# Cross-attention, eight sequences on one core: half of the partition swaps of quads 24 to 56 issued by GpSimd

## The chip, the cores and the metric

The kernel runs on one core of a Trainium2 chip. The metric is device time in microseconds of one execution; three runs of the kernel before gave 575.96, 576.25 and 576.99, a median of 576.25 us.

The engines are named here as in the profile: PE is TensorE (matmuls; PEld is its weight loads), DVE is VectorE, ACT is ScalarE, POOL is GpSimd, SP is SyncE, which in this kernel only issues transfers (its queue is SPq).

## The reference

Everything is float32. A layer norm of x, a projection to queries, attention of 32 heads of width 32 over 256 keys, an output projection and the residual. Keys and values are both the context itself, without a projection.

```python
mu = mean(x); var = variance(x)                      # x: (8, 256, 1024)
h = (x - mu) * rsqrt(var + 1e-5) * gamma + beta
Q = split_heads(h @ Wq.T)                            # 32 heads of 32
K = split_heads(ctx); V = split_heads(ctx)           # ctx: (8, 256, 1024)
scores = einsum('bhsd,bhtd->bhst', Q, K) * 32 ** -0.5
probs = softmax(where(mask, scores, -inf))
attn = einsum('bhst,bhtd->bhsd', probs, V)
out = x + merge_heads(attn) @ Wout.T
```

## The kernel before

**Quads.** The work of attention is cut into 64 quads: sequence b (0 to 7) times group (0 to 7) of four heads, numbered n = 8 b + group. One pass of the main loop, step n, puts on TensorE: the scores of quad n + 1 (L486), the values of quad n - 2 (L629), and between and behind them the query projection of a later sequence (L447, from the fourth sequence on in seven products per sequence, Strassen-like) and steps of the output projection of an earlier one (L715). It then emits the softmax of quad n + 1 (`softmax_parts`). The order of instructions on each engine is the order in which the program is written; each engine executes its own list in that order and waits on semaphores.

**One softmax.** For each of the four heads j of a quad: `exps(j)` is bias, minimum over the row on VectorE (L522) and exponential with row sum on ScalarE (L526), for two halves of the rows each; `normalize(j)` is a reciprocal of the row sums on VectorE (L533) and two scalings of 128 x 256 on GpSimd (L535); `blocks(j)` is one transpose in blocks of 32 x 32 on VectorE (L541), which writes the head's part of the tile pT. VectorE works through the reciprocals and transposes of one quad before the bias and minimum of the next, so the scalings on GpSimd stand between them.

**The swaps.** Blocks of 32 x 32 transposed in place leave the keys of two neighbouring groups of 32 partitions in the wrong halves. So partitions 32 to 63 of half 0 have to change places with partitions 0 to 31 of half 1, and 96 to 127 with 64 to 95. `aside(0)` and `aside(1)` on ScalarE (L547) copy half 1 of pT to a tile pc, two heads at a time; then, in `tail()`, two transfers of 128 KB inside the on-chip memory overwrite half 1 from half 0 (L607, "pT<-pT"), and two more write half 0 from pc (L611, "pT<-pc"). The first two wait for the second copy aside; each of the other two waits for the landing of the first of its pair, which reads what it overwrites. Loads that happen to be due (`between`: keys, residual rows, kept weights, the next x) are issued between the two pairs. All of this goes through SyncE's queue, which waits in order. pT has three buffers, pc two; the scores have four banks, one quad's worth, so the scores of quad n + 1 need the bias and minimum of quad n done.

**What else GpSimd does.** Behind the scalings of a quad stand, in the order of the program: sums for the query products (`sum_x`, L437), sums for the output products (`sum_at`, L691), additions to the residual (`add_p1`, L748; `add_kept` near the end), and small layer norm steps (L239, L249). In the first sequences it also folds gamma into the weights and forms weight sums (L366, L185, L398).

**Where tails are deferred.** In the first eight quads and in quads 57 to 62, `tail()` runs after the next quad's first exponentials; in quads 8 to 56, and 63, directly behind the scalings.

Of the kernel before, what the change touches and what calls it, by code (L numbers as in the profile page):

```python
# [59 lines left out]
def xattn_kernel(  # L60
# [11 lines left out]
    nc = tc.nc  # L72
# [4 lines left out]
    NQ = NC  # L77
# [4 lines left out]
    K = 32  # L82
# [4 lines left out]
    N = B * NQ  # L87
# [403 lines left out]
    def softmax(*args):  # L491
        for _ in softmax_parts(*args):
            pass

    tails = []


    def softmax_parts(n, copies=(), ahead=(), between=(), hooks={}, fill=()):

        fill = list(fill)

        def fill_in():
            if fill:
                fill.pop(0)()

        pss = scs[n]  # L510
        pT = pTs[n] = ptp.tile([P, 2, NI, NH, NS, K], F32, tag="pT", name=f"pT_{n}")
        pc = asp.tile([P, NI, NH, NS, K], F32, tag="pc", name=f"pc_{n}")
        es, mns, dens = {}, {}, {}

        def exps(j, part=range(NS)):
            if 0 in part:
                es[j] = ep.tile([P, NS, T], F32, tag="e", name=f"e_{n}_{j}")
                mns[j] = sm.tile([P, NS], F32, tag="mn", name=f"mn_{n}_{j}")
                dens[j] = sm.tile([P, NS], F32, tag="den", name=f"den_{n}_{j}")
            e, mn, den = es[j], mns[j], dens[j]  # L520
            for s in part:
                nc.vector.tensor_tensor_reduce(  # L522
                    out=e[:, s, :], in0=pss[j][:, s, :], in1=mbs[n // NQ], scale=1.0,
                    scalar=NO_SCORE, op0=ALU.add, op1=ALU.min, accum_out=mn[:, s : s + 1],
                )
                nc.scalar.activation(  # L526
                    e[:, s, :], e[:, s, :], AF.Exp, bias=mn[:, s : s + 1], scale=-1.0,
                    accum_out=den[:, s : s + 1],
                )

        def normalize(j):
            rden = sm.tile([P, NS], F32, tag="rden", name=f"rden_{n}_{j}")
            nc.vector.reciprocal(rden, dens[j])  # L533
            for s in range(NS):
                nc.gpsimd.tensor_scalar(  # L535
                    es[j][:, s, :], es[j][:, s, :], rden[:, s : s + 1], 1.0,
                    ALU.mult, ALU.mult,
                )

        def blocks(j):  # L540
            nc.vector.transpose(  # L541
                pT[:, :, :, j, :, :].rearrange("p a i s k -> p (a i) s k"),
                es[j].rearrange("p s (b t) -> p b s t", t=K),
            )

        def aside(j):
            nc.scalar.copy(pc[:, :, ts(j, 2)], pT[:, 1, :, ts(j, 2)])  # L547

        if n == 0:
            for j in range(NH - 1):  # L550
                exps(j, (0,))
            yield
            exps(NH - 1, (0,))
            fill_in()
            yield
            for j in range(NH):
                exps(j, (1,))
            normalize(0)
            fill_in()
        else:  # L560
            exps(0)
            while tails:
                tails.pop()()
            late = "p1" in hooks
            if not late:
                for done in list(pvs):
                    copy_at(done)
            exps(1)
            for hook in hooks.get("soon", ()):
                hook()  # L570
            exps(2)
            normalize(0)
            for hook in hooks.get("p1", ()):
                hook()
            exps(3)
            if late:
                for done in list(pvs):
                    copy_at(done)
        if n <= NQ:
            for copy in copies:  # L580
                copy()
        for hook in hooks.get(0, ()):
            hook()
        normalize(1)
        fill_in()
        blocks(0)
        for hook in hooks.get(1, ()):
            hook()
        normalize(2)
        fill_in()  # L590
        blocks(1)
        aside(0)
        normalize(3)
        fill_in()
        blocks(2)
        while fill:
            fill_in()
        if n > NQ:
            for copy in copies:
                copy()  # L600

        def tail():
            blocks(3)
            aside(1)

            for r in range(2):
                nc.sync.dma_start(pT[ts(2 * r, K), 1], pT[ts(2 * r + 1, K), 0])  # L607
            for load in between:
                load()
            for r in range(2):  # L610
                nc.sync.dma_start(pT[ts(2 * r + 1, K), 0], pc[ts(2 * r, K)])  # L611

        for load in ahead:
            load()
        if n < NQ or N - NQ < n < N - 1:
            tails.append(tail)
        else:
            tail()
        yield
# [16 lines left out]
    def copy_at(n):  # L636
        b, c = divmod(n, NQ)
        k, c = divmod(c, NK)
        if c == 0:
            ats[b, k] = atp.tile([P, NK, NS, NA, K], F32, tag="at", name=f"at_{b}_{k}")  # L640
        for r, pv in enumerate(pvs.pop(n)):
            nc.scalar.copy(
                ats[b, k][:, c, :, ts(r, 2), :], pv.rearrange("p a s k -> p s a k")
            )
# [243 lines left out]
    for c in range(NC):  # L888
        copy_x0(1, c, nc.scalar if c < NC // 2 else nc.vector)
    first = softmax_parts(0, (partial(copy_q, 1), partial(copy_q, 2)), (), (), {}, [  # L890
        partial(ln_stats, 1, 0), partial(ln_stats, 1, 1),
        partial(ln_norm, 1, 0, nc.vector),
# [14 lines left out]
    for b in range(B - 1):  # L907
        done, ends = 0, b == B - 2
        for i, counts in enumerate(steps_of(b)):
            n = NQ * (b + 1) + i  # L910
# [227 lines left out]
```

## Time and profile before

| | |
|---|---|
| median of three runs | 576.25 us |
| profiled execution, span | 577.0 us |
| TensorE busy | 567.3 us, 98% |
| VectorE busy | 460.4 us, 80% |
| ScalarE busy | 411.7 us, 71% |
| GpSimd busy | 409.8 us, 71% |
| DMA queue of SyncE | 110.40 MB, 66.8% of 16 DMA engines' span |
| DMA queue of GpSimd | not in the profile |

The span runs from the first to the last instruction of the profiled execution, which was 0.75 us longer than the median of the runs. Busy time counts instructions that compute; issuing a transfer, semaphore and register instructions are not in it. A timeline row gives start and duration in us, engine, line, operation, output and input tiles (buffer numbers left out), shape, how many instructions were merged into the row (x8), and in brackets the idle time in front of it with what ended it. A row by stretches gives, for each engine, busy time and number of instructions, then the granted TensorE clock (1.00 is full), the DMA engines' busy share and GB/s. A row of waits reads: who waited, for whom, total us, times, longest.

### The profile page before, as it was taken

Reading aid. Unit: us, or ns where it says so; the run is one execution under the profiler, and the core shown is the slowest. Engines: PE = TensorE matmul, PEld = TensorE weight load, DVE = VectorE, ACT = ScalarE, POOL = GpSimd, SP = SyncE. Lnnn points to the kernel's source line nnn. Section 1 sums busy time; section 2 is a strip of 40 time slices with the busy share of each in tenths; the row PEclk is TensorE's granted clock in tenths of the full one; section 3 lists DMA queues with packets and bytes.
Section 4 is the critical chain, followed back from the end, with each engine's and each line's share of the span. In section 5 each row is a group of like instructions: output and inputs, shape, how many; then the busy total and the mean of one; then the engine's idle time right before and its main releaser. Section 6 shows DMA issues by size and latency. Waiting matters only on the chain. (4 is left out here: it accounts for less than half of the span.)

```text
span 577.0 us, 20128 instructions
## 1 busy us (share of the span) xinstructions
PE 567.3 (98%) x7162; PEld 394.2 (68%) x7162; DVE 460.4 (80%) x1695; ACT 411.7 (71%) x1425; POOL 409.8 (71%) x677
## 2 busy tenths in 40 slices
PE   8999998999999999999999999999999999999997
PEld 8788784667667777677676677667766767755543
DVE  5888887788877879979888788988878878779823
ACT  4697886677667877688677867768767776769810
POOL 1778898889896896876568675676658657448770
PEclk9999999899999999999999999999999999999999
DMA  8974766656677777957678856687567864446751
GB/s 304 394 206 126 208 161 180 192 148 166 185 220 222 200 208 207 271 166 201 188 213 228 211 138 189 212 240 206 148 161 236 224 170 130 130 138 178 199 166 73
DMA packets 50100, 111.69 MB, mean 194 GB/s; under 512 B 9424, under 2 KB 10192, under 8 KB 50000
## 3 DMA queue, kind: packets, MB, share of 16 engines
q1 hardware_dynamic: 49712, 110.40, 66.8%
q8 instruction: 57, 0.93, 0.7%
q14 instruction: 43, 0.35, 0.2%
q10 hardware_dynamic: 288, 0.01, 0.0%
HBM read 60.04 MB, written 10.49 MB: 122 GB/s over the span
## 5 line engine op out<-in xcount | busy, mean ns | idle before, releaser
L535 POOL TENSOR_SCALAR e<-e,rden 128x256 f32<-128x256 f32 x512 | 236.0, 478 | 116.9 <-DVE rden L533 114.4
L526 ACT ACTIVATE e<-e,mn 128x256 f32<-128x256 f32 x512 | 253.9, 501 | 50.7 <-DVE mn L522 49.6
L541 DVE STREAM_TRANSPOSE pT<-e 128x512 f32<-128x512 f32 x256 | 180.9, 707 | 44.7 <-POOL e L535 32.7
L522 DVE CUSTOM_DVE_ANT_0 e<-sc,mb 128x256 f32<-128x256 f32 x512 | 185.4, 416 | 26.4 <-PE sc L486 26.0
L547 ACT COPY pc<-pT 128x512 f32<-128x512 f32 x128 | 79.0, 617 | 72.1 <-DVE pT L541 36.6
L526 ACT ACTIVATION_READ_ACCUMULATOR e<-e,mn 128x1 f32 x512 | 97.9, 191 | 0.0
L345 PE MATMUL pq<-xnT,wq 128*128 128x256 f32 (+1 forms) x368 | 84.1, 383 | 0.6 <-ACT qa L354 0.6
L345 PEld LDWEIGHTS pq<-xnT,wq 128*128 128x128 f32 x368 | 68.9, 190 | 15.4 <-issue 3.7
L629 PE MATMUL pv<-pT,v 64*32 64x128 f32 x4096 | 74.7, 274 | 3.5 <-DMA v<-in_kv_dram 2.9
L629 PEld LDWEIGHTS pv<-pT,v 64*32 64x32 f32 x4096 | 57.5, 105 | 26.7 <-issue 14.7
L486 PEld LDWEIGHTS sc<-k,qa 32*128 32x128 f32 x1024 | 46.2, 184 | 41.9 <-issue 23.6
L715 PE MATMUL po_S<-wo,at 128*128 128x512 f32 x152 | 74.3, 606 | 0.0
L486 PE MATMUL sc<-k,qa 32*128 32x256 f32 x1024 | 73.6, 401 | 0.1
L715 PE MATMUL po_A<-wo,at 128*128 128x512 f32 x128 | 61.2, 620 | 0.3 <-ACT qa L354 0.3
L715 PE MATMUL po_S<-wo,s 128*128 128x512 f32 x104 | 49.9, 606 | 0.0
L533 DVE RECIPROCAL rden<-den 128x2 f32<-128x2 f32 x256 | 37.6, 147 | 7.7 <-ACT e L526 6.8
L522 DVE DVE_READ_ACCUMULATOR2_ANT mn<- 128x1 f32 x512 | 42.5, 83 | 0.0
L715 PEld LDWEIGHTS po_A<-wo,at 128*128 128x128 f32 x128 | 23.4, 193 | 26.2 <-issue 24.5
L447 PEld LDWEIGHTS pq_A<-xnT,wq 128*128 128x128 f32 x320 | 37.3, 192 | 4.8 <-issue 3.6
L715 PEld LDWEIGHTS po_S<-wo,at 128*128 128x128 f32 x152 | 25.8, 190 | 19.7 <-issue 19.1
L447 PE MATMUL pq_A<-xnT,wq 128*128 128x128 f32 x320 | 37.3, 275 | 0.0
L748 POOL TENSOR_TENSOR r<-r,p 128x512 f32<-128x512 f32 x23 | 29.4, 1278 | 7.1 <-DMA r<-in_x_dram 3.3
(96 smaller groups left out, 608.7 us busy)
## 6 DMA issues: line engine op xcount, KB each, us to landing
v<-in_kv_dram SPq DMA_DIRECT2D x64, 256.0 KB, 3.9
pT<-pT SPq DMA_DIRECT2D x128, 128.0 KB, 3.1
pT<-pc SPq DMA_DIRECT2D x128, 128.0 KB, 3.5
ring<-kept_T SPq DMA_DIRECT2D x18, 512.0 KB, 5.2
k<-in_kv_dram SPq DMA_DIRECT2D x32, 256.0 KB, 3.1
x<-in_x_dram SPq DMA_DIRECT2D x14, 512.0 KB, 5.1
r<-in_x_dram SPq DMA_DIRECT2D x28, 256.0 KB, 5.1
out_dram<-r SPq DMA_DIRECT2D x28, 256.0 KB, 3.0
```

Source lines behind the costliest of these rows:

```text
L345: nc.tensor.matmul(pqs[n], wq[:, o, c, :], xnTs[b](c), start=(c == 0), stop=(c == NC - 1),)
L447: nc.tensor.matmul(pqs[b][:, o, :], w[:, c], x_[:, c], start=begins and o + c == 0, stop=c == NK - 1, skip_group_check=True,)
L486: nc.tensor.matmul(scs[n][j][:, s, :], qa[r, n % NQ, ts(s, P)], ks[n - n % 2][r, n % 2, :], start=True, stop=True,)
L522: nc.vector.tensor_tensor_reduce(out=e[:, s, :], in0=pss[j][:, s, :], in1=mbs[n // NQ], scale=1.0, scalar=NO_SCORE, op0=ALU.add, op1=ALU.m ...
L526: nc.scalar.activation(e[:, s, :], e[:, s, :], AF.Exp, bias=mn[:, s : s + 1], scale=-1.0, accum_out=den[:, s : s + 1],)
L533: nc.vector.reciprocal(rden, dens[j])
L535: nc.gpsimd.tensor_scalar(es[j][:, s, :], es[j][:, s, :], rden[:, s : s + 1], 1.0, ALU.mult, ALU.mult,)
L541: nc.vector.transpose(pT[:, :, :, j, :, :].rearrange("p a i s k -> p (a i) s k"), es[j].rearrange("p s (b t) -> p b s t", t=K),)
L547: nc.scalar.copy(pc[:, :, ts(j, 2)], pT[:, 1, :, ts(j, 2)])
L629: nc.tensor.matmul(pvs[n][r][j * HD : (j + 1) * HD], vs[n][ts(r, 2 * K), i, ts(j, HD)], pT[ts(r, 2 * K), :, i, j, :, :], start=(i == 0), s ...
L715: nc.tensor.matmul(po, operand(b, name)[:, c], wo[:, which, c], start=begins and c == 0, stop=c == NK - 1, skip_group_check=not begins,)
L748: nc.gpsimd.tensor_tensor(r, r, p1s[b], ALU.add)
```

## The change

In `tail()` the four swaps become calls of a helper `swap(r, back, engine)`: r is the pair (0: partitions 0 to 63, 1: partitions 64 to 127), `back` tells the write of half 0 from pc from the write of half 1 from half 0. Pair 0 stays on SyncE's queue at the same places. For quads 24 to 56 pair 1 is issued by GpSimd: its first swap at the place in the program where SyncE's stood, so in GpSimd's order directly behind the quad's last scaling and ahead of the sums and additions of that step; its second swap is put into a list and issued in the next quad's softmax, in GpSimd's order between the two scalings of `normalize(0)` and those of `normalize(1)`. In all other quads both pairs go through SyncE as before. 66 transfers change their queue; number and size of transfers, and everything on TensorE, VectorE and ScalarE, stay in the same order.

```diff
     tails = []
+    shared = []
+    FIRST_SHARED, LAST_SHARED = 3 * NQ, N - NQ + 1
...
             exps(2)
             normalize(0)
+            while shared:
+                shared.pop()()
             for hook in hooks.get("p1", ()):
                 hook()
             exps(3)
...
             aside(1)
 
-            for r in range(2):
-                nc.sync.dma_start(pT[ts(2 * r, K), 1], pT[ts(2 * r + 1, K), 0])
+            def swap(r, back, engine):
+                to, of = (pT[ts(2 * r + 1, K), 0], pc[ts(2 * r, K)]) if back else (
+                    pT[ts(2 * r, K), 1], pT[ts(2 * r + 1, K), 0]
+                )
+                engine.dma_start(to, of)
+
+            second = nc.gpsimd if FIRST_SHARED <= n < LAST_SHARED else nc.sync
+            swap(0, False, nc.sync)
+            swap(1, False, second)
             for load in between:
                 load()
-            for r in range(2):
-                nc.sync.dma_start(pT[ts(2 * r + 1, K), 0], pc[ts(2 * r, K)])
+            swap(0, True, nc.sync)
+            if second is nc.sync:
+                swap(1, True, second)
+            else:
+                shared.append(partial(swap, 1, True, second))
```

NQ is 8 and N is 64, so `FIRST_SHARED` is 24 and `LAST_SHARED` 57.

## The prediction

> **What bounds the kernel now.** I read the waits and the busy time by stretches first, since they say whether anything but TensorE sets the end, then one quad's timeline on each engine, then the rows that price the moved transfers. The stretch in which quads 24 to 56 are scaled and swapped runs from about 217 to 500 us; inside it I take two batches of eight quads each.
>
> ```profile
> core 0: us, PE busy (x) PEld busy (x) DVE busy (x) ACT busy (x) POOL busy (x), PEclk, DMA share, GB/s
> 217.00:500.00 283.00, 282.15 (x3871) 200.02 (x3878) 236.39 (x870) 210.84 (x740) 189.30 (x327) 1.00 0.70 195
> ...
> 284.82:352.75 67.93, 67.93 (x922) 48.06 (x921) 58.21 (x213) 51.39 (x179) 45.96 (x81) 1.00 0.73 200
> 421.70:489.63 67.93, 67.93 (x922) 48.06 (x921) 53.36 (x203) 49.21 (x177) 44.38 (x77) 1.00 0.67 189
> ...
> PE pv L629 <- DMA v<-in_kv_dram: 0.9, 1, 0.9
> ```
>
> TensorE is busy for 282.15 of 283.00 us, at a granted clock of 1.00, and waited once, 0.9 us, for a load of v. Both batches take exactly 67.93 us, all of it TensorE's. So in this stretch nothing can be won beyond 0.85 us; the change can only keep TensorE fed or starve it. GpSimd has 67.93 - 45.96 = 21.97 us to spare in the first batch. The question is what the change does with that spare time.
>
> One quad, quad 34, whose scores TensorE makes at 300.98, shows where it lies. Engine by engine, in the order GpSimd, VectorE, ScalarE, SyncE's queue, TensorE:
>
> ```profile
> 304.62 3.92 POOL L535 TENSOR_SCALAR e<-e,rden 128x256 f32<-128x256 f32 x8 [0.78 <-DVE rden L533]
> 308.50 1.27 POOL L691 TENSOR_TENSOR s<-at,at 128x512 f32<-128x512 f32 x1
> 309.74 1.26 POOL L437 TENSOR_TENSOR xnT<-xnT,sx 128x512 f32<-128x512 f32 x1
> ...
> 313.56 3.67 POOL L535 TENSOR_SCALAR e<-e,rden 128x256 f32<-128x256 f32 x8
> ...
> 308.57 0.71 DVE L541 STREAM_TRANSPOSE pT<-e 128x512 f32<-128x512 f32 x1 [0.27 <-POOL e L535]
> ...
> 313.27 0.42 DVE L522 CUSTOM_DVE_ANT_0 e<-sc,mb 128x256 f32<-128x256 f32 x1
> ...
> 309.32 0.62 ACT L547 COPY pc<-pT 128x512 f32<-128x512 f32 x1 [1.01 <-DVE pT L541]
> ...
> 309.96 1.14 SPq L607 DMA_DIRECT2D pT<-pT  x2
> ...
> 314.70 1.14 SPq L611 DMA_DIRECT2D pT<-pc  x2
> ...
> 316.04 1.88 PE L715 MATMUL po_S<-wo,s 128*128 128x512 f32 x4
> 317.86 1.15 PE L486 MATMUL sc<-k,qa 32*128 32x256 f32 x16
> ...
> 328.30 1.16 PE L629 MATMUL pv<-pT,v 64*32 64x128 f32 x64
> ```
>
> The eight scalings end at 308.54. The last transpose and the copy aside end at 309.28 and 309.94, and only then may the first swap be issued: 1.40 us after the last scaling, the "turn". During the turn GpSimd now goes straight on with its additions (308.50, 309.74). The last bias-and-minimum of quad 35, at 313.27 + 0.42 = 313.69, frees the last score bank; TensorE writes the next scores at 317.86. So the softmax chain may come 4.17 us late before TensorE feels it, once; whatever it loses after that, TensorE loses too.
>
> **The change, part by part.** *Work moved to GpSimd.* For each of 33 quads two transfers of 128 KB leave SyncE's queue for GpSimd's. Bytes are the same. Before, SyncE takes 1.14 us for two such issues, 0.57 each.
>
> GpSimd has no transfer in this trace, so its price S for issuing one has to be bounded. GpSimd's additions, its smallest instruction and the landing of these swaps:
>
> ```profile
> L607 SPq DMA_DIRECT2D pT<-pT x68: 507/582/1892, 218.7 to 499.6; - x68
> DMA to landing us min/median/max: 2.2/3.4/6.5
> ...
> 295.00 0.55 POOL L239 TENSOR_TENSOR rstd<-ve,mhalf 128x1 f32<-128x1 f32 x1 [2.43 <-DVE ve L236]
> 317.20 0.26 POOL L249 TENSOR_SCALAR shift<-mv,rstd 128x1 f32<-128x1 f32 x1
> 317.42 1.27 POOL L691 TENSOR_TENSOR at<-at,s 128x512 f32<-128x512 f32 x1
> 321.43 0.93 POOL L535 TENSOR_SCALAR e<-e,rden 128x256 f32<-128x256 f32 x2 [2.73 <-DVE rden L533]
> 335.12 1.27 POOL L748 TENSOR_TENSOR r<-r,p 128x512 f32<-128x512 f32 x1
> 351.94 1.27 POOL L691 TENSOR_TENSOR at<-at 128x512 f32<-128x512 f32 x1
> ```
>
> The low end is GpSimd's smallest instruction, 0.26 us (one value a partition); the high end its dearest, 1.27. The nearest row is the same transfer's issue on SyncE, 0.57, and a GpSimd instruction also pays its own start, for which the 0.26 stands: I take 0.57 + 0.27 = 0.84 us, an estimate from these two rows. [...]
>
> *The first swap on GpSimd, and the wait in front of it.* It stands directly behind the last scaling in GpSimd's order and waits for the copy aside. GpSimd executes in order, so each quad's additions, and behind them the next quad's scalings, queue behind the turn: 1.40 us in which GpSimd used to work or wait for something else, plus S.
>
> *The swap back, behind the next quad's first scaling.* It costs S again, and it waits for the first swap to land. SyncE's swaps land a median 3.4 us after their issue starts; with the dearer issue 3.4 + 0.27 = 3.67. On GpSimd's side S, the quad's additions X and a pair of scalings (0.93) pass meanwhile: 1.77 + X. With two or three additions the landing is covered. It is not in four quads of the batch: that with X = 0.55 (row at 295.00) waits 1.35, those with X = 1.27 (335.12, 351.94) 0.63 each, that with 0.26 + 1.27 (317.20, 317.42) about 0.41, together 3.0. Queued behind that wait are the other six scalings, and behind them VectorE's transposes.
>
> *The sum for a batch of eight.* GpSimd's own work 45.96, eight turns 11.20, sixteen issues 13.44, landing waits 3.0: 73.6 us against TensorE's 67.93. GpSimd becomes the bound, by 5.7 us per batch. Quads 24 to 47 are three such batches (189.30 us in 283 is 45.4 per 67.93, so the shown one is no outlier): 17.1. Quads 48 to 55 have 1.58 us less on GpSimd (44.38): 4.1. Quad 56 adds an eighth of a batch, 0.7. Together 21.9, less the 4.17 that the chain may be late: 17.7 us. The profiled execution spans 577.0 us, 0.75 above the median of the runs, 576.25; put on the median, 576.25 + 17.7 = 594.0.
>
> *What is late next.* When the chain is late it is VectorE's bias-and-minimum that frees the score banks late, so TensorE waits at the scores (L486). The sums for the products have about as much room: the one made at 308.50 is used at 316.04, 6.3 us after its end, and would be made 1.40 + 0.84 = 2.2 us later, leaving 4.0. The values are not late: SyncE's second swap back for quad 34 is issued at about 315.3, lands near 318.7, and TensorE reads it at 328.30; GpSimd's would land 1 to 2 us later plus the lag.
>
> *SyncE's queue.* It is spared 66 issues of 0.57, 38 us. What it waited for is here:
>
> ```profile
> SPq L607 <- ACT pc L547: 44.7, 18, 5.1
> SPq L611 <- DMA pT<-pT: 39.9, 32, 2.9
> ```
>
> Both waits stay, since the other half's swaps stay there; loads behind them go up to 1.14 us earlier. Costed at a gain of nothing, as TensorE's only wait for a load is the 0.9 above; with it the gain is 0.9. The buffers hold: three of pT, two of pc, and the next use of pc is two quads (17 us) on.
>
> **The rivals.**
> 1. *GpSimd's issue is no dearer than SyncE's*: the batch is then 60.2 + 16 S, and up to S = 0.55 it exceeds 67.93 by no more than 1.0, which the 4.17 covers over 33 quads: 576.3. At 0.57 the sum is still within a few tenths. For it: GpSimd's smallest instruction is only 0.26. Against it: 0.55 is below SyncE's own price for the same transfer.
> 2. *GpSimd's issue costs 1 us or more*: at 1.0 the batch is 76.2 and the time 604; at 1.27, the dearest instruction that GpSimd has here, 80.5 and about 622. Against it: 1.27 is the price of 512 elements on all partitions.
> 3. *VectorE holds the issue up*: if each issue waited for one VectorE instruction, 0.42 us as at 313.27, S would be 1.26 and the time about 621. Against it: the eight scalings take 3.67 to 3.92 us beside running VectorE work. [...]
> 4. *Faster*: SyncE's relief brings the load of v in time, 0.9 us, 575.4. It decides only if S stays under 0.55; and the 0.85 us of idle TensorE leave no room for more than 0.2% (1.15 us, about what a measurement of this kernel can tell from no change), unless TensorE's instructions get shorter.
>
> **How the numbers follow.** My forecast, S between 0.55 and 1.0, gets 0.40 with its own range 577 to 604; rival 1 0.21; rival 2 0.26; rival 3 0.08; rival 4 beyond 0.2% 0.05. Slower is 0.40 + 0.26 + 0.08 = 0.74, the same 0.21, faster 0.05. The range goes down to 575.4 (the 0.9 us) and up to 612 (S = 1.12), which leaves out the dear half of rivals 2 and 3, about 0.17, and little below.
>
> **What would show it.** Right: two transfer issues per quad on GpSimd of 0.7 to 1.0 us; the additions starting some 2.2 us after the last scaling instead of at once; GpSimd's wait for VectorE's reciprocals (L533), 2 to 3 us in most quads, mostly gone; VectorE's wait for scores gone and TensorE waiting at the scores for VectorE from about quad 30 on; batches of 70 to 75 us instead of 67.93. Wrong: batches still of 67.93 with issues under 0.55; or the lag showing on the values instead, which would mean a landing far beyond 6.5 us; or issues over 1 us, where the mechanism holds and the price fails.

## The result, and the profile after

The changed kernel takes 600.12 us (median of four runs, 598.80 to 602.72) against 576.11 for the kernel before: a ratio of 1.0417, 95% interval 1.0381 to 1.0452. That is 24.0 us slower; the forecast was 594.0, range 575.4 to 612. The profiled execution took 600.83 us, 0.7 above the median; its span, from the first to the last instruction, is 599.1, that is 1.7 less. The 577.0 us given ahead of the prediction is a span too, so by an estimate from this difference that execution took about 578.7 us and stood 2.5 above its median instead of 0.75.

First the busy time of the page of the kernel after and its stretches (columns as in the prediction: busy time and number of instructions for each engine, granted clock, DMA share, GB/s). 214.13 to 521.85 us holds the work that stood between 217 and 500 us before, the stretch in which the swaps are shared (both ends shifted by the starts of the same quads' scores); 287.18 to 362.61 runs from the scores of quad 32 to those of quad 40, the batch that took 67.93 us before; the last two rows are a wait of TensorE and what follows it.

```profile
PE 572.9 (96%) x7162; PEld 394.4 (66%) x7162; DVE 458.6 (77%) x1695; ACT 412.1 (69%) x1425; POOL 445.5 (74%) x743
```

```profile
214.13:521.85 307.72, 289.90 (x3870) 201.55 (x3878) 234.81 (x870) 211.57 (x740) 224.01 (x391) 0.98 0.63 179
287.18:362.61 75.43, 70.23 (x922) 48.59 (x921) 58.04 (x213) 51.62 (x180) 54.57 (x97) 0.98 0.65 183
320.00:323.20 3.20, 0.11 (x2) 0.00 (x0) 1.81 (x11) 3.10 (x13) 3.20 (x5) 0.93 0.31 84
323.20:326.60 3.40, 3.35 (x7) 1.19 (x7) 2.29 (x6) 0.86 (x3) 3.35 (x8) 0.57 0.63 193
```

For the same work TensorE now needs 307.72 us instead of 283: it idles 17.82 us where it idled 0.85, and is busy for 289.90 instead of 282.15. The batch takes 75.43 us; the prediction said 73.6. GpSimd is busy 54.57 us in it instead of 45.96, and the 8.61 more are sixteen issues of 0.54, which the profile, other than with SyncE's issues, counts as busy time (x97 instead of x81).

What GpSimd waited for in that batch, and its rows around the end of quad 34 and the start of quad 35 (timeline: start, duration, engine, line, operation; in brackets the idle time ahead and what ended it):

```profile
POOL pT L614 <- ACT pc L549: 12.3, 7, 2.0
POOL e L537 <- DVE rden L535: 3.5, 3, 1.6
POOL pT L614 <- DMA v<-in_kv_dram: 2.0, 1, 2.0
POOL pT L614 <- DMA pT<-pT: 1.8, 2, 1.1
```

```profile
317.64 0.54 POOL L614 DMA_DIRECT2D pT<-pT  x1 [1.69 <-ACT pc L549]
318.21 1.29 POOL L705 TENSOR_TENSOR s<-at,at 128x512 f32<-128x512 f32 x1
319.45 1.26 POOL L437 TENSOR_TENSOR xnT<-xnT,sx 128x512 f32<-128x512 f32 x1
320.67 0.56 POOL L239 TENSOR_TENSOR rstd<-ve,mhalf 128x1 f32<-128x1 f32 x1
321.21 1.26 POOL L762 TENSOR_TENSOR r<-r,p 128x512 f32<-128x512 f32 x1
322.46 0.93 POOL L537 TENSOR_SCALAR e<-e,rden 128x256 f32<-128x256 f32 x2
323.34 0.60 POOL L614 DMA_DIRECT2D pT<-pc  x1
323.99 2.75 POOL L537 TENSOR_SCALAR e<-e,rden 128x256 f32<-128x256 f32 x6
```

The first swap waits 1.69 us for the copy aside, the turn. It adds up over the batch to 14.3 us (12.3, and 2.0 put down to a load at the same place). Busy 54.57, turns 14.3 and landings 1.8, the terms of the prediction's sum, make 70.7 of the 75.43 us. The rest is 3.9 us of other waits, 3.5 of them for VectorE's reciprocals (18.2 before), and small gaps. So GpSimd has little slack left, but its own list does not fill the batch. Where does TensorE feel the delay? Its own waits in the kernel after, from 217 to 530 us:

```profile
PE po_S L729 <- DVE r L771: 14.2, 7, 3.1
PE po_A L729 <- DVE qa L463: 2.0, 2, 1.2
PE sc L486 <- DVE qa L468: 1.2, 3, 0.4
```

Not at the scores (1.2 us), but at the output products, L729, for VectorE's store L771 that empties the bank of an earlier product. One of the seven waits, on VectorE and TensorE:

```profile
322.50 0.69 DVE L771 TENSOR_TENSOR r<-po_A,r 128x512 f32<-128x512 f32 x1 [1.39 <-POOL r L762]
...
316.38 3.73 PE L447 MATMUL pq_S<-sx,ring 128*128 128x128 f32 x32
323.25 3.41 PE L729 MATMUL po_S<-wo,s 128*128 128x512 f32 x4 [3.13 <-DVE r L771]
326.58 1.15 PE L486 MATMUL sc<-k,qa 32*128 32x256 f32 x16
```

GpSimd adds to the residual (L762, 321.21 to 322.47), the last of the four instructions that queue behind the turn and the issue; VectorE's store waits 1.39 us for that; TensorE's products wait 3.13 us for the store, so VectorE would have been late without the addition too. Then the four products take 3.41 us instead of the 1.88 of the prediction's row at 316.04, since the clock granted in 323.20 to 326.60 is 0.57. Three such stores in the kernel before, each with the product behind it (the product of the second row is that row at 316.04):

```profile
247.21 0.69 DVE L757 TENSOR_TENSOR r<-po_A,r 128x512 f32<-128x512 f32 x1 [1.44 <-POOL r L748]
...
313.62 0.69 DVE L757 TENSOR_TENSOR r<-po_A,r 128x512 f32<-128x512 f32 x1
...
348.23 0.69 DVE L757 TENSOR_TENSOR r<-po_S,r 128x512 f32<-128x512 f32 x1
...
248.12 1.88 PE L715 MATMUL po_S<-wo,s 128*128 128x512 f32 x4
...
350.08 2.74 PE L715 MATMUL po_S<-wo,s 128*128 128x512 f32 x6
```

The room there is 248.12 - 247.90 = 0.22, 316.04 - 314.31 = 1.73 and 350.08 - 348.92 = 1.16 us. Such a store stands ahead of quads 28, 36, 44 and 52 (room 0.22, 1.73, 0.68 and 1.59 us in this trace) and ahead of quads 32, 40 and 48 (1.16 or 1.17): these are the seven waits of 14.2 us. At quad 28 the store already waited 1.44 us for the addition before the change.

Setting the starts of each quad's scores in the two traces against each other, TensorE falls behind by 3.6, 4.8, 3.4 and 4.5 us at quads 28, 36, 44 and 52, by 1.4, 1.1 and 1.9 at 32, 40 and 48, and by 24.7 in all from quad 22 on (up to there the trace after is 2.9 us ahead); behind quad 52 by nothing more. So 20.7 of the 24.7 us come at the seven stores, longer products behind three of them included. The rest has other places: 0.7 each at 33, 41 and 49, where TensorE waits 0.41 us for VectorE in the middle of the scores ahead (sc <- qa above), and 0.9 at 35, where it waits for VectorE at po_A.

### The profile page after: what moved, and what is told of

It is laid out like the page before. It is cut to its first block, busy times and chain, and to the rows that moved or that the text cites. A ratio compares the mean times of both kernels' runs of the same rounds, so it can differ in the third digit from the quotient of the medians.

```text
span 599.1 us, 20193 instructions
## 1 busy us (share of the span) xinstructions
PE 572.9 (96%) x7162; PEld 394.4 (66%) x7162; DVE 458.6 (77%) x1695; ACT 412.1 (69%) x1425; POOL 445.5 (74%) x743
## 4 chain that ended last, share of the span: by engine, by line
PE 55%; POOL 18%; DVE 10%; DMA 7%; issue 5%; ACT 3%; SPq 1%; POOLq 0%; DVEq 0%; ACTq 0%
PE po_S L729 13%; POOL e L537 10%; PE pq L345 9%; PE pq_A L447 8%; PE sc L486 7%; PE pv L643 6%; PE po_A L729 6%; DVE e L524 4%; DVE pT L543 3%; DMA pT<-pT 3%; ACT e L528 2%; DMA v<-in_kv_dram 2%; PE po_end L796 2%; POOL pT L614 2%; PE pq_S L447 2%
## 5 line engine op out<-in xcount | busy, mean ns | idle before, releaser
L549 ACT COPY pc<-pT 128x512 f32<-128x512 f32 x128 | 78.9, 617 | 98.5 <-issue 43.4
L345 PEld LDWEIGHTS pq<-xnT,wq 128*128 128x128 f32 x368 | 68.7, 190 | 14.3 <-issue 4.1
L729 PE MATMUL po_S<-wo,at 128*128 128x512 f32 x152 | 74.5, 607 | 0.2 <-DVE r L767 0.2
L729 PE MATMUL po_S<-wo,s 128*128 128x512 f32 x104 | 55.1, 660 | 14.2 <-DVE r L771 14.2
L614 POOL DMA_DIRECT2D pT<-pT x33 | 17.9, 543 | 59.0 <-ACT pc L549 57.0
L729 PE MATMUL po_A<-wo,at 128*128 128x512 f32 x128 | 59.5, 605 | 2.2 <-DVE qa L463 2.0
L535 DVE RECIPROCAL rden<-den 128x2 f32<-128x2 f32 x256 | 37.3, 146 | 13.3 <-ACT e L528 12.1
L729 PEld LDWEIGHTS po_A<-wo,at 128*128 128x128 f32 x128 | 22.9, 189 | 27.7 <-issue 24.0
L729 PEld LDWEIGHTS po_S<-wo,s 128*128 128x128 f32 x104 | 19.2, 202 | 33.1 <-issue 16.8
L729 PEld LDWEIGHTS po_S<-wo,at 128*128 128x128 f32 x152 | 25.8, 190 | 20.2 <-issue 19.5
```

The source lines that it names most:

```text
L345: nc.tensor.matmul(pqs[n], wq[:, o, c, :], xnTs[b](c), start=(c == 0), stop=(c == NC - 1),)
L614: engine.dma_start(to, of)
L729: nc.tensor.matmul(po, operand(b, name)[:, c], wo[:, which, c], start=begins and c == 0, stop=c == NK - 1, skip_group_check=not begins,)
```

## The experiments

No kernel here leaves out work of the reference. A loss is the ratio less 1, times 576 us. "The first swap" and "the back swap" are those of partitions 64 to 127 in quads 24 to 56. Lines carry each kernel's own numbers: the first swap's and back swap's line is L614 or L616, the copy aside L547 or L549, the addition to the residual and VectorE's store move likewise.

### One of the two moves alone

The back swap left to SyncE:

```diff
-            second = nc.gpsimd if FIRST_SHARED <= n < LAST_SHARED else nc.sync
...
-            if second is nc.sync:
-                swap(1, True, second)
-            else:
-                shared.append(partial(swap, 1, True, second))
+            swap(1, True, nc.sync)
```

> Only the first swap (half 1 of partitions 64 to 127) is issued by GpSimd, the swap back stays on SyncE. Theory A (the loss comes from the turn: GpSimd stands still until the copy aside, the addition of P1 behind it comes late, VectorE's store of the first result block waits for that addition, and TensorE waits for the bank): nearly the whole loss of the changed kernel remains, 592 to 600 us. Theory B (the loss comes from GpSimd's issuing time, 0.55 us for each of 66 transfers): half of it goes, about 588. Theory C (my prediction's sum, GpSimd's total of work, turns and issues): one issue of 0.55 us per quad less, 33 x 0.55 = 18 us less, about 582.

585.51 us, 1.0174 (1.0148 to 1.0201): a loss of 10.0. None of the three theories had this time: it lies between B's and C's.

The first swap left to SyncE, the back swap behind the next quad's first scalings as in the change:

```diff
-            swap(1, False, second)
+            swap(1, False, nc.sync)
```

> Only the swap back is issued by GpSimd, behind the next quad's first scaling; the first swap stays on SyncE, so GpSimd doesn't wait for the copy aside. Theory A: the loss goes nearly, 576 to 579 us. Theory B: half of it stays, about 588. Theory C: GpSimd's sum for eight quads is 46 + 8 x 0.55 = 50 us against TensorE's 67.9, so the loss goes, 576.

595.94 us, 1.0345 (1.0272 to 1.0418): a loss of 19.9. Each half alone loses much; their sum, 29.9, is above the 24.0 of both, so the second kernel did something that the change does not. All three theories had expected 576 to 588 us. TensorE's longest waits and GpSimd's wait for the landing in it (217 to 530 us):

```profile
PE po_A L729 <- DVE qa L463: 8.1, 4, 3.0
...
POOL pT L614 <- DMA pT<-pT: 17.8, 14, 2.8
```

The back swap now waits 17.8 us for SyncE's first swap to land, where the changed kernel waits 8.6 in the same window; another 16.4 us of idle time ahead of it are put down to other engines, so the wait may be up to twice as long. So it is no clean half of the change: it prices a landing wait in the middle of a quad's scalings. TensorE feels this one mostly at other places, 8.1 us at po_A and 4.6 at the scores, both for VectorE's qa, and only 2.5 at the stores.

### The wait without the issue

All swaps on SyncE; GpSimd makes a copy of one value a partition (0.18 us) from the tile of the copy aside, at the first swap's place:

```diff
             aside(1)
+            if 3 * NQ <= n < N - NQ + 1:
+                nc.gpsimd.tensor_copy(gs[:, :1], pc[:, NI - 1, NH - 1, NS - 1, K - 1 : K])
```

> All swaps on SyncE as before the change; at the place of the first swap GpSimd copies one value per partition out of the copy aside's output, so it only waits there, for about 0.3 us of work. Theory A: the additions come 1.7 us (the wait) plus 0.3 late instead of 1.7 plus 0.55, and half or more of the loss stays, 586 to 596 us. Theories B and C: no transfer is issued by GpSimd, eight turns of 1.7 us fit into its spare time (46 + 13.6 + 2.4 = 62 us of 67.9), 576 to 577.

576.88 us, 1.0033 (1.0010 to 1.0057): a loss of 1.9. The turn is there in full, 53.6 us over 33 quads, and most of it goes into time that GpSimd had waited for reciprocals (88.5 us in this window before, 41.3 here):

```profile
POOL gs L606 <- ACT pc L547: 53.6, 33, 2.1
POOL e L535 <- DVE rden L533: 41.3, 41, 4.7
...
PE po_S L717 <- DVE r L759: 2.5, 3, 1.3
```

The last row is TensorE's: its waits at the output products are there already, but small. The time is the one of theories B and C; A, by which the turn alone costs 586 to 596, is wrong.

### Is it the addition to the residual?

The largest wait came behind that addition, at the quads 28, 36, 44 and 52, each of which is scored behind the softmax of quad 26, 34, 42 or 50. First those four quads were given back to SyncE:

```diff
-            second = nc.gpsimd if FIRST_SHARED <= n < LAST_SHARED else nc.sync
+            second = nc.gpsimd if FIRST_SHARED <= n < LAST_SHARED and n % NQ != 2 else nc.sync
```

> As the changed kernel, but the four quads whose swap stands ahead of the addition of P1 to the first result block (26, 34, 42, 50) keep all swaps on SyncE. Theory A: the four lags of 3.4 to 4.8 us that TensorE shows right behind them go, and with them their cause, 580 to 585 us. Theories B and C: 29 of 33 quads still pay, 29/33 of 24 us, about 597.

591.72 us, 1.0283 (1.0258 to 1.0309): a loss of 16.3, 7.7 less than the change. The lag at quads 28, 36, 44 and 52 fell to 0.7, 1.9, 1.9 and 0.5 us, but 1.9 each remain at 32, 40 and 48. The time lies between the 580 to 585 of theory A and the 597 of the others.

Then the addition itself was taken off GpSimd:

```diff
-        nc.gpsimd.tensor_tensor(r, r, p1s[b], ALU.add)
+        engine = nc.vector if (s, h) == (0, 0) and b > 1 else nc.gpsimd
+        engine.tensor_tensor(r, r, p1s[b], ALU.add)
```

> As the changed kernel, but the addition of P1 to the first result block, which VectorE's store waits for, is done by VectorE itself from the third sequence on (one addition of 0.7 us in a batch of eight quads), so it no longer queues behind GpSimd's swap. Theory A (that store is the place where TensorE loses most, 3.4 to 4.8 us once per batch): those four lags shrink to 1 to 2 us, 586 to 591 us. Theory C (GpSimd's total is the bound): only 1.27 us less for GpSimd per batch, 595 to 597.

604.49 us, 1.0475 (1.0431 to 1.0518): worse still, and above both forecasts. The lags at the same four quads are 4.4, 5.1, 5.1 and 3.6. TensorE's largest wait stays, with another name, and VectorE's addition and the store behind it show why this kernel settles less than it was built for:

```profile
PE po_S L729 <- DVE rden L535: 12.9, 4, 3.4
```

```profile
318.88 1.69 DVE L763 TENSOR_TENSOR r<-r,p 128x512 f32<-128x512 f32 x1
...
321.93 0.68 DVE L772 TENSOR_TENSOR r<-po_A,r 128x512 f32<-128x512 f32 x1
```

The expectation gave the addition 0.7 us on VectorE; it takes 1.69 here, and 1.68 to 3.28 at the four places, ahead of the very stores that TensorE waits for. So the edit took one delay off GpSimd and put another into VectorE's list. It shows that the lag doesn't need the addition in GpSimd's order; what the lag would be with the addition free of cost, it doesn't show. In the change the store of the first such wait shown waits 1.39 of TensorE's 3.13 us for the addition. For the rest VectorE itself comes late: its transposes wait 41.5 us for GpSimd's scalings between 217 and 530 us, where they waited 16.9 before.

### The same transfers at other places

First both later: the first swap ahead of the next quad's first scalings, where the copy aside is long done, and the back swap behind that quad's last scaling:

```diff
-    shared = []
+    shared, backs = [], []
...
             exps(2)
-            normalize(0)
             while shared:
                 shared.pop()()
+            normalize(0)
...
+        while backs:
+            backs.pop()()
...
-            swap(1, False, second)
+            if second is nc.sync:
+                swap(1, False, second)
+            else:
+                shared.append(partial(swap, 1, False, second))
...
-                shared.append(partial(swap, 1, True, second))
+                backs.append(partial(swap, 1, True, second))
```

> Same 66 transfers on GpSimd, but the first swap stands behind the step's additions, just ahead of the next quad's first scaling, and the swap back behind the next quad's last scaling. Theory A with its extension (it is the places of the two issues: the turn in front of the additions, the swap back inside the chain of scalings): the copy aside and the landing are over when GpSimd comes to them, 575 to 578 us. Theory B (the issuing time as such, 0.55 us each): 590 or more still.

575.69 us, 1.0007 (0.9983 to 1.0030): no loss, as expected, with the same 66 transfers on GpSimd. The stretch of this kernel, its GpSimd waits and TensorE's one wait at the output products:

```profile
217.00:500.00 283.00, 282.63 (x3868) 199.93 (x3865) 238.15 (x875) 211.66 (x746) 221.59 (x391) 1.00 0.70 195
```

```profile
PE po_S L734 <- DVE r L776: 0.4, 1, 0.4
```

```profile
POOL pT L616 <- DMA pT<-pT: 6.3, 6, 2.3
POOL pT L616 <- ACT pc L549: 2.4, 2, 1.2
```

The turn is down from 57.0 us to 2.4. GpSimd is busy for nearly as long as in the changed kernel (221.59 us here, 224.01 there, 391 instructions each), so neither the issuing time nor the transfers as such cost anything here.

Then one of the two places at a time. The first swap as in the change, the back swap behind the next quad's last scaling:

```diff
-                shared.append(partial(swap, 1, True, second))
+                backs.append(partial(swap, 1, True, second))
```

> First swap as in the changed kernel (behind the last scaling, the turn in front of it), swap back behind the next quad's last scaling, where GpSimd waits for the copy aside anyway. If the turn and the swap back inside the scalings add up: what is left is that of the first swap alone, as in the run with the first swap only on GpSimd (10.5 us over before): 584 to 588 us. If the swap back alone carries the loss: 577.

584.92 us, 1.0151 (1.0105 to 1.0197): a loss of 8.7, as expected about that of the first swap alone. TensorE's waits at the output products are 7.2 us in all, the longest 1.3, and GpSimd's turn is 39.9 us, 17 less than in the change: the back swap's issue lies inside the turn of the next quad now.

The first swap ahead of the next quad's first scalings, the back swap right behind them:

```diff
             exps(2)
+            while shared:
+                shared.pop()()
             normalize(0)
+            while backs:
+                backs.pop()()
```

> First swap behind the step's additions, ahead of the next quad's first scaling, swap back behind that scaling as in the changed kernel: no turn in front of the additions, but the landing (2.9 us after the issue in the changed kernel's trace) now falls between the first and the second pair of scalings, a wait of about 1.5 us in each quad beside the issue of 0.55. If delays inside the chain of scalings are what costs: 590 to 600 us, as with the swap back alone on GpSimd (595.9). If the turn is: 577 to 580.

610.00 us, 1.0561 (1.0496 to 1.0625): a loss of 32.3, more than the 590 to 600 us expected. Only two scalings (0.93 us) now lie between the swap and its return, so GpSimd stands in the middle of its scalings until the swap has landed:

```profile
POOL pT L616 <- DMA pT<-pT: 43.2, 23, 4.0
```

The four kernels side by side, loss in us:

| | back swap between the scalings | back swap behind the last scaling |
|---|---|---|
| first swap directly behind its quad's last scaling | 24.0 (the change) | 8.7 |
| first swap ahead of the next quad's first scaling | 32.3 | 0.4, within the measurement |

### The landing waits of the changed kernel

The change itself has 8.6 us of landing waits between 217 and 530 us. To see whether they matter, the back swap was put behind the second pair of scalings instead of the first:

```diff
-            normalize(0)
-            while shared:
-                shared.pop()()
...
+            while shared:
+                shared.pop()()
```

(the lower place is behind `normalize(1)`).

> As the changed kernel, but the swap back stands behind the next quad's second pair of scalings instead of the first, 0.93 us later: its wait for the landing (8.0 us in total in the changed kernel) should nearly go, its issue of 0.55 us stays inside the chain of scalings. If the landing waits make the difference of 15 us between the changed kernel and the run with the swap back behind the last scaling: 585 to 590 us. If it is the issue inside the chain, on top of the turn: 596 to 600.

600.05 us, 1.0426 (1.0389 to 1.0462): a loss of 24.5, the same as the change, with the landing waits gone:

```profile
POOL pT L614 <- ACT pc L549: 57.2, 32, 2.0
POOL e L537 <- DVE rden L535: 20.6, 26, 1.7
...
POOL pT L614 <- DMA pT<-pT: 1.1, 2, 0.8
```

The 7.5 us that no longer go into landings go into waits for reciprocals (20.6 here, 13.3 in the change). So at this place it isn't the landing that costs; what is left is the issue itself between a quad's scalings, on top of the turn.

### The time without the transfers

All swaps on SyncE, and behind the first scalings of quads 25 to 57 an instruction of GpSimd as long as the back swap's issue, 0.55 us (a power of one value a partition):

```diff
             normalize(0)
+            if 3 * NQ < n <= N - NQ + 1:
+                nc.gpsimd.tensor_tensor(gs[:, :1], gam[:, :1], mhalf[:, :1], ALU.pow)
```

> All swaps on SyncE as before the change; behind the first pair of scalings of quads 25 to 57 GpSimd does one small power on one value per partition, which takes 0.55 us as in the layer norm. No turn, no landing, no transfer: the time of one issue inside the chain of scalings, alone. If a delay of 0.55 us is within the room that the chain has where TensorE waits for nothing (0.2 to 1.7 us at VectorE's stores): 576 to 579 us. If every such delay adds up: 576 + 33 x 0.55 = 594.

577.28 us, 1.0032 (1.0008 to 1.0057): a loss of 1.8. Then this and the turn together; behind the waiting copy stands a small scaling, so that wait, copy and scaling take the place of the first swap:

```diff
             aside(1)
+            if 3 * NQ <= n < N - NQ + 1:
+                nc.gpsimd.tensor_copy(gs[:, 1:2], pc[:, NI - 1, NH - 1, NS - 1, K - 1 : K])
+                nc.gpsimd.tensor_scalar(gs[:, 2:3], gam[:, 1:2], gam[:, :1], -1.0, ALU.mult, ALU.mult)
```

> All swaps on SyncE as before the change, but GpSimd's time as in the changed kernel: behind the last scaling it waits for the copy aside and does about 0.45 us of work on one value per partition (a copy of 0.18, a scaling of 0.26), and behind the next quad's first pair of scalings the small power of 0.55. No transfer on GpSimd. If the delays in GpSimd's order are the whole cause, and only together exceed the room at VectorE's stores: 590 to 600 us. If the transfers themselves (their landing, their queue, SyncE's waits for them) are needed for the loss: no more than the sum of the two parts measured alone, 1.9 + 1.8 us over before, 577 to 581.

587.20 us, 1.0205 (1.0157 to 1.0254): a loss of 11.8, without one transfer on GpSimd, between the two forecasts of 577 to 581 and 590 to 600. TensorE waits at the same place as in the change; the second row is the batch from the scores of quad 32 to those of quad 40:

```profile
PE po_S L720 <- DVE r L762: 7.2, 7, 1.2
```

```profile
284.14:355.62 71.48, 68.90 (x921) 48.26 (x921) 57.98 (x213) 51.67 (x180) 53.42 (x105) 1.00 0.70 197
```

The turn alone lost 1.9 us and the instruction between the scalings 1.8; together, and with the 0.2 us that the small scaling adds behind the turn, they lose three times that sum. How the 11.8 us divide between the two places isn't shown: the first swap alone on GpSimd, with 0.56 us behind the turn and nothing between the scalings, already lost 10.0. In both readings a delay costs little up to some size and much beyond it, as it would with a room that is used up. And GpSimd's work and turns (12.9 us by its waits) are 53.42 + 12.9 = 66.3 us in this batch, less than TensorE's 67.93 before; still the batch takes 71.48.

Last, the same with a third small instruction behind the wait, so that from the wait's end to the additions it is 0.50 us, and four small copies in place of the power:

```diff
+                nc.gpsimd.tensor_copy(gs[:, 3:4], gam[:, 3:4])
...
-                nc.gpsimd.tensor_tensor(gs[:, :1], gam[:, :1], mhalf[:, :1], ALU.pow)
+                for c in range(4, 8):
+                    nc.gpsimd.tensor_copy(gs[:, c : c + 1], gam[:, c : c + 1])
```

> As the run without transfers on GpSimd before it, but with the lengths of the changed kernel: about 0.55 us behind the wait for the copy aside (was 0.4 from start to next start) and 0.60 us behind the first pair of scalings (four small copies, was 0.53). All swaps on SyncE. If GpSimd's delays are the whole cause, 0.15 to 0.3 us more per quad over 33 quads adds 5 to 10 us, and the halved clock comes back where TensorE waits longest: 592 to 600 us. If the transfers have a part of their own: still about 587.

589.49 us, 1.0226 (1.0191 to 1.0261): a loss of 13.0, of the change's 24.0, and below the 592 to 600 us expected if GpSimd's delays were all. GpSimd in this kernel:

```profile
316.09 0.18 POOL L609 COPY gs<-pc 128x1 f32<-128x1 f32 x1 [1.46 <-ACT pc L547]
...
316.59 1.27 POOL L698 TENSOR_TENSOR s<-at,at 128x512 f32<-128x512 f32 x1
...
321.69 0.55 POOL L575 COPY gs<-gam 128x1 f32<-128x1 f32 x4
322.20 1.86 POOL L535 TENSOR_SCALAR e<-e,rden 128x256 f32<-128x256 f32 x4
```

From last scaling to additions, and again between the scalings, GpSimd loses 1.46 + 0.50 + 0.51 = 2.47 us here; in the changed kernel's rows it is 1.69 + 0.57 + 0.65 = 2.91. By the medians of the 33 quads (1.53, 0.50 and 0.51 against 1.70, 0.56 and 0.60) the difference is smaller, 0.32, or 10.6 us of GpSimd in all. TensorE's halved clock (below) costs the change about 4.8 us more, which this kernel does not have. The two together could cover the 11.0 us that are missing, but they weren't taken apart, and a part of the transfers' own isn't excluded.

Set side by side, the kernels that delay GpSimd at these two places fall into nearly one order, with transfers or without. The delay is an estimate from the traces: idle time in front and the time up to GpSimd's next instruction, over the 33 quads. 1.8 us a quad (the wait alone) lost 1.9 us, 2.3 and 2.4 (the back swap behind the last scaling, the first swap alone) 8.7 and 10.0, 2.6 and 2.7 (the last two, without transfers) 11.8 and 13.0, 3.0 and 3.2 (the back swap behind the second scalings, and the change) 24.5 and 24.0. Only where the landing wait itself stands in the middle of the scalings (19.9 and 32.3) was more lost. So it is shown that waiting and issuing time at these two places lose 13 us without any transfer, and that the transfers lose nothing at other places; how the last 11 us are made up stays open.

## Why the prediction was right, and where it was wrong

**The bound.** TensorE had nothing to win: right. No kernel here was faster than before; the cheapest, with both swaps later, measured 1.0007.

**Work moved: the price S.** Too dear. I took 0.84 us, SyncE's 0.57 and 0.27 for GpSimd's own start. The issue rows of the kernel after (minimum, median, maximum in ns) show no such addition:

```profile
L614 POOL DMA_DIRECT2D pT<-pT x33: 536/536/758, 223.5 to 522.0; - x33
L614 POOL DMA_DIRECT2D pT<-pc x32: 536/558/605, 227.2 to 517.0; - x32
```

0.54 to 0.56, just the price of rival 1, at which that rival said "no change". The price came true and its time did not: by its sum the batch would have been 60.2 + 16 x 0.55 = 69.0 us and the chain's room would have covered the rest. So the distance of 6.1 us from forecast to result is the rest of errors of opposite sign, not a price that was nearly right. Rivals 2 and 3 needed issues of 1 us and over, and fell with these rows. No run shows the price of 1.0 us with which rival 2 begins and my own range, 577 to 604, ends: the longest of the 66 issues of the kernel after took 0.76 us, and the means in the other runs are 0.50 to 0.57. With both swaps later, the same 66 transfers left the DMA engines' share from 217 to 500 us at 0.70 and their rate at 195 GB/s, as before the change.

**The first swap and its wait.** The mechanism was right: the wait for the copy aside stands in GpSimd's order and the additions and next scalings queue behind it. Its size was 1.7 to 1.8 us instead of 1.40, that is 14.3 in the batch instead of 11.2.

**The landing waits.** Predicted 3.0 in a batch, measured 1.8, and by the kernel with the back swap behind the second scalings they make no difference to the time.

**The sum.** 73.6 predicted and 75.43 measured, which looks closer than it is. The issues took 8.6 instead of 13.44, the turns 14.3 instead of 11.2, the landings 1.8 instead of 3.0: with these the prediction's sum is 70.7, 2.8 above 67.93, and carried through as in the prediction (three batches, a lighter one, an eighth, less 4.17) it gives about 582 us. So 18 us of the loss are not in the sum, and that the forecast of 594.0 came so near is luck: too dear a price made up for what it left out. GpSimd came close to its limit (its waits for reciprocals became few, as said), but the sum of its list isn't what decides: without transfers the list was 66.3 us long in the batch, under TensorE's 67.93, and 11.8 us were lost.

**What is late next, and the room of 4.17 us.** This is the step that failed. I took the room at the scores, 4.17 us, called the sum's room, 4.0, "about as much", and subtracted it once. TensorE waits 1.2 us at the scores and 14.2 at the output products, for VectorE's store of the block before, which the sum left out. There the room was 0.22 to 1.73 us, at two places of every batch. What TensorE loses at one such place isn't given back, and in the same batch there is a next one. So delays far under 4 us already cost time: the turn and 0.56 us of issue behind it lose 10.0 us. "From about quad 30 on" was nearly so: the first loss, 3.6 us, is at quad 28.

**SyncE's queue.** A gain of nothing: right. Its waits grew rather than shrank, 82.9 us for the copy aside (44.7 before) and 44.3 for the landing (39.9), and here the copies are late for SyncE's half as well:

```profile
SPq L614 <- ACT pc L549: 82.9, 21, 5.7
SPq L614 <- DMA pT<-pT: 44.3, 32, 3.8
```

Lateness isn't all of it: with both swaps later, where TensorE loses nothing, the two waits are 63.4 and 57.6 us. SyncE has 66 issues less to make there too and may simply come to its waits earlier; the two were not separated.

## What to carry to other kernels

What the issues cost on GpSimd, whose rows run in the order of the program, was decided in this kernel by where they stood: the same 66 transfers lost 32 us, 24 us, 9 us or nothing. An issue that waits belongs behind work which doesn't need it and at a place where what it waits for is done; GpSimd's idle time, 29% of the span, said nothing about that. And the room of a chain is read at every consumer of each engine behind it, the stores that empty a bank among them, and counted anew in each round.

## What the hardware showed that I had not expected

**Half the clock after some waits.** Three of TensorE's waits in the kernel after were followed by about 3.5 us at a granted clock of 0.54 to 0.57, in which four products lasted 3.4 to 3.6 us instead of 1.88: about 4.8 us in all. The waits were 1.87, 3.13 and 2.58 us long. The first of them and one wait without it, from the timeline, and the clock in the stretches behind the first, the third and the one without:

```profile
247.28 3.46 PE L729 MATMUL po_S<-wo,s 128*128 128x512 f32 x4 [1.87 <-DVE r L771]
...
399.06 1.98 PE L729 MATMUL po_S<-wo,s 128*128 128x512 f32 x4 [3.14 <-DVE r L771]
```

```profile
247.20:250.70 3.50, 3.42 (x8) 0.99 (x8) 2.33 (x7) 0.88 (x3) 3.45 (x8) 0.56 0.73 205
473.06:476.65 3.59, 3.59 (x8) 1.24 (x8) 2.37 (x7) 1.15 (x4) 3.39 (x8) 0.54 0.57 183
399.00:402.40 3.40, 3.34 (x44) 1.75 (x52) 2.30 (x7) 0.85 (x3) 3.35 (x8) 1.00 0.61 191
```

Behind an idle time of 1.87 us the granted clock was 0.56, behind one of 3.14 us it was 1.00. So the length of the wait alone does not decide it here; what does is not shown.

**The swaps on GpSimd were about as fast as SyncE's.** GpSimd is held for 0.54 to 0.56 us, SyncE for 0.57; from issue to landing it takes a median 2.9 us for the first swap and 3.8 for the back swap (SyncE's before, between 217 and 500 us: 3.3 and 3.6).

**The swap began a little later than a small copy.** Behind the end of the copy aside the swap began after 0.29 us, a small copy that waited for the same thing after 0.13 (medians of 33 each, the changed kernel and the last one without transfers).
